# The order of VectorE's work in the second Y phase: weight rests behind the pair's work

## The chip, the cores and the metric

The kernel runs on one core of a Trainium2 chip. The metric is device time in microseconds. Several runs are taken and their median is compared; a run with the profiler gives the trace.

Five engines work beside each other, each in its own order: TensorE (PE) multiplies matrices, VectorE (DVE) and ScalarE (ACT) work element by element, GpSimd (POOL) issues some of the transfers and does a few small operations, SyncE (SP) issues most of the transfers. Semaphores make one engine wait for another or for a transfer.

## The reference, cut to what matters

Two batches of 1024 rows with 1024 columns go through a layer normalization, two products and a gate. `S` is a product with a block-sparse weight, `Y` a product with a dense weight plus a mix of eight low-rank terms whose coefficients come from the mean over the rows:

```python
xn = layernorm(x)
s = xn @ (weight * block_mask).T + bias
coeffs = softmax((mean_over_rows(xn) @ Wq.T) @ lora_keys.T / sqrt(128))
y = xn @ (W_org.T + sum_e coeffs[e] * down[e] @ up[e])
out = x + s * silu(y)
```

## The kernel before, in words

**Precision.** Every float32 operand of a product is kept as two parts: the part rounded to the type that TensorE multiplies (written by ScalarE, `hi`) and the rest, operand minus rounded part (written by VectorE, `lo`). A product is three matmuls: hi by hi, hi by lo, lo by hi. The *rest* of this document's title is the `lo` part of a block of the S weight.

**Stages.** Batch 0 is computed in the plain way: S's left half, Y's left half (phase `("y", 0, 0)`), Y's right half (phase `("y", 0, 1)`, the *second Y phase*, 157 to 204 us), then S's right half in eight tiles (`s_tile`), mixed with *folds*, which make the Y weight of batch 1. Batch 1 is computed with a scheme of seven products in place of eight on 2 by 2 blocks (from about 291 us to the end); it needs sums and differences of blocks of the normalized input, made ahead of time and stored in DRAM (`xv`).

**The second Y phase.** TensorE computes eight tiles of 128 rows, 24 matmuls each (`gemm`, L450 to L454). Beside it three other tasks run, which the generator `jobs_c(i)` hands out tile by tile:

- *S weight, right half*, eight blocks `kt` of 128 by 512. `s_mul` (L294 to L303): SyncE loads the block into a stage tile `ws` (L297), VectorE multiplies it by the block mask (L299), ScalarE writes the rounded part into `slot` (L302). `s_lo` (L305 to L307): VectorE writes the rest, block minus rounded part, into `slot` (L307); this frees the stage tile. The result, `s1`, is first used by `s_tile(0)`.
- *Pairs of blocks of batch 1's input*. `wide_load` (L958) loads two blocks in a pair `j`; `wide_norm` subtracts the row means (L962) and scales, while it sums each row (L963, sums into `xsum`); `wide_a(j)` normalizes the first half, `wide_b(j)` the second half and then forms four differences (L968), whose stores to `xv` GpSimd issues (L524). Pair 0 and half of pair 1 belong to the phase before; `wide_b(1)`, `wide_a(2)`, `wide_b(2)`, `wide_a(3)`, `wide_b(3)` to tiles 0 to 4 of this phase. Pair 3 uses the tiles of pair 1 again.
- *The coefficients of batch 1* (`coeffs(1)`, four steps). `steps[0]`, `sums`: eight transposes of `xsum` on TensorE (L322), behind the matmuls of tile 5. `steps[1]`, `query`: VectorE multiplies the sums by `Wq` (L346) and makes `qb` (L350). `steps[2]`, `scores`: TensorE multiplies `qb` by the keys (L357); this stands in the middle of tile 6 (`split_at`), between its first twelve matmuls and the rest; then VectorE begins the softmax (L359 to L362). `steps[3]` ends it, and `scale_up` scales the low-rank factors for the folds (L389 to L393).

**What sets the order.** TensorE, VectorE, ScalarE and GpSimd run exactly in the order in which the program is written (`manual_schedule`). SyncE is not in that list: a planner orders its loads. A load waits in its queue until its tile is free, and what is behind it waits too. Stage tiles come from one pool of six (`tag="st"`), which `ws`, the fourth difference of a pair (`xt`) and the fold's loads (`ds`, `wo`, `us`) share. `unit_load` (L1081) loads batch 1's first unit of weights into `raw`, parts of which hold the row means and pair 2's second half in this phase.

Of the kernel before, what the change touches and what calls it, by code (L numbers as in the profile page):

```python
# [32 lines left out]
def kernel(  # L33
# [258 lines left out]
    def new_slot():  # L292
        return wpool.tile([P, NKT, 2, NH], F32R, name="slot", tag="w")
# [257 lines left out]
    J = lambda f, *a: (lambda: f(*a))  # L551
# [98 lines left out]
    with tc.manual_schedule(engines={mybir.EngineType.PE, mybir.EngineType.DVE, mybir.EngineType.Activation, mybir.EngineType.Pool}):  # L650
# [343 lines left out]
        s1 = new_slot()  # L994
        steps = coeffs(1)

        def jobs_c(i):
            if i < 2:
                yield J(store_out, 1 - i)
            if i == 5:  # L1000
                yield steps[0]
                yield steps[1]
            if i == 6:
                yield steps[3]
                yield J(scale_up, 1, 0, up_homes)
            if i < 6:
                yield J(s_mul, s1, 1, i)
                yield J(s_lo, s1, 1, i)
            if i == 5:
                for kt in (6, 7):  # L1010
                    yield J(s_mul, s1, 1, kt)
                    yield J(s_lo, s1, 1, kt)
            if i in (0, 2):
                yield J(wide_load, 2 + i // 2, 0)
                yield J(wide_load, 2 + i // 2, 1)
            if i < 5:
                yield J((wide_b, wide_a)[i % 2], 1 + (i + 1) // 2)

        up_homes = [misc[:, 0, :]]
        split_at[(0, 1, 6)] = steps[2]  # L1020
        phase("y", 0, 1, y01, False, jobs_c)


# [341 lines left out]
```

## Time and profile before

| | us |
|---|---|
| three runs, median (lowest to highest) | 453.02 (452.56 to 454.11) |
| the profiled execution | 451.54 |
| its span, first to last instruction | 449.8 |
| TensorE busy (98% of the span) | 439.7 |
| VectorE busy (64%) | 289.4 |
| ScalarE busy (39%) | 175.6 |
| GpSimd busy (17%) | 76.6 |
| from 186 to 198 us: TensorE busy, of 12 | 10.25 |
| from 186 to 198 us: VectorE busy, of 12 | 10.23 |

The page and the views give each instruction's line in the kernel, its engine, its tiles (output, arrow, inputs), its start and its duration. A bracket behind a row of the timeline is the idle time of that engine just before, and what ended it. In the list of waits a row reads: the waiting instruction, an arrow, what it waited for, then the total, the number of times and the longest. The granted clock of TensorE was 1.00 in every stretch of the second Y phase. Matmul durations overlap (a matmul of 512 columns is shown as 0.39 us long, but the next starts 0.23 us after it).

### The profile page before, as it was taken

To read this page: it belongs to the slowest core of one execution; us is meant where nothing else is said; L and a number is where in the kernel's file an instruction comes from. 1 tells how busy PE (TensorE), PEld (TensorE's weight loads), DVE (VectorE), ACT (ScalarE), POOL (GpSimd) and SP (SyncE) were. 2 spreads that over 40 slices of the span, in tenths; PEclk is the share of its full clock that TensorE was granted. 3 is DMA by queue.
4 is the path that set the end of the run, shared out by engine and by line. 5 is a ranking of instruction groups with operands and counts; after the bars stand their busy time and mean duration, and the time that the engine had idled before them with its cause. 6 is when DMAs were issued, how large, how long until landed. Compare 5 with 4: busy or idle time off the path is not lost.

```text
span 449.8 us, 5786 instructions
## 1 busy us (share of the span) xinstructions
PE 439.7 (98%) x2058; PEld 363.3 (81%) x2058; DVE 289.4 (64%) x478; ACT 175.6 (39%) x291; POOL 76.6 (17%) x93
## 2 busy tenths in 40 slices
PE   7999999999999999999999999999999999999996
PEld 5789888888888888778888788888888888888885
DVE  5989777766528758876456667487556294365615
ACT  3676626454631221225233134067344322441520
POOL 3784210002220402221000000110020030002000
PEclk9999999999999999999999999999999999999999
DMA  8995406687796887797979797966183146218103
GB/s 272 390 345 207 143 25 206 215 265 217 250 306 179 267 248 251 268 346 259 286 219 311 218 306 197 302 176 189 40 180 127 66 110 172 93 24 209 49 1 117
DMA packets 47741, 90.58 MB, mean 201 GB/s; under 512 B 4816, under 2 KB 15328, under 8 KB 47712
## 3 DMA queue, kind: packets, MB, share of 16 engines
q1 hardware_dynamic: 30624, 66.08, 43.1%
q0 software_dynamic: 6624, 16.26, 15.7%
q10 hardware_dynamic: 10464, 7.87, 5.4%
q8 instruction: 16, 0.26, 0.3%
q14 instruction: 13, 0.11, 0.1%
HBM read 70.26 MB, written 19.93 MB: 201 GB/s over the span
## 4 chain that ended last, share of the span: by engine, by line
PE 73%; issue 10%; DMA 8%; DVE 4%; POOL 3%; SPq 0%; ACT 0%; POOLq 0%; DVEq 0%; ACTq 0%
PE acc_ps L1211 25%; PE py L1211 10%; PE acc_ps L450 8%; PE acc_ps L454 8%; PE acc_ps L453 8%; PE psw L416 5%; PE psw L415 5%; PE psw L414 5%; DMA ramp<-in_wT_dram 2%; DMA keys_sb<-in_keysT_dram 2%; POOL xv L524 2%; DMA ramp<-in_mask_dram 2%; DMA misc<-in_up_dram 1%; DMA xv<-xt 1%; POOL stash L502 1%
## 5 line engine op out<-in xcount | busy, mean ns | idle before, releaser
L1211 PE MATMUL acc_ps<-xw,ow 128*128 128x512 f32 (+1 forms) x492 | 113.2, 386 | 0.0
L1211 PEld LDWEIGHTS acc_ps<-xw,ow 128*128 128x128 f32 x492 | 91.0, 188 | 19.5
L450 PE MATMUL acc_ps<-slot,xgrp 128*128 128x512 f32 (+1 forms) x288 | 106.6, 370 | 0.1
L454 PE MATMUL acc_ps<-slot,xgrp 128*128 128x512 f32 (+1 forms) x288 | 105.7, 367 | 0.7 <-DVE xgrp L603 0.7
L453 PE MATMUL acc_ps<-slot,xgrp 128*128 128x512 f32 (+1 forms) x288 | 105.7, 367 | 0.6 <-DVE slot L591 0.2
L453 PEld LDWEIGHTS acc_ps<-slot,xgrp 128*128 128x128 f32 x288 | 54.3, 189 | 10.8 <-DVE slot L591 2.1
L454 PEld LDWEIGHTS acc_ps<-slot,xgrp 128*128 128x128 f32 x288 | 54.2, 188 | 10.2 <-DVE xgrp L603 1.1
L450 PEld LDWEIGHTS acc_ps<-slot,xgrp 128*128 128x128 f32 x288 | 54.3, 189 | 9.1 <-DVE stash L466 0.3
L416 PE MATMUL psw<-cut,dlo 128*128 128x512 f32 x128 | 50.1, 391 | 0.3 <-DVE dlo L406 0.3
L414 PE MATMUL psw<-cut,dhi 128*128 128x512 f32 x128 | 49.9, 390 | 0.0
L415 PE MATMUL psw<-cut,dhi 128*128 128x512 f32 x128 | 49.8, 389 | 0.0
L1211 PE MATMUL py<-xw,ow 128*128 128x512 f32 x192 | 46.9, 392 | 0.0
L1211 PEld LDWEIGHTS py<-xw,ow 128*128 128x128 f32 x192 | 36.1, 188 | 7.9
L1104 DVE TENSOR_TENSOR ow<-raw,ow 128x1024 fp32r<-128x1024 f32 (+1 forms) x32 | 34.5, 1088 | 9.9 <-ACT ow L1103 9.9
L405 ACT CAST dhi<-ds 128x512 fp32r<-128x512 f32 x32 | 19.7, 616 | 40.8 <-DMA ds<-in_down_dram 25.2
L502 POOL DMA_DIRECT2D stash<-in_x_dram x16 | 14.4, 899 | 117.6 <-DVE stash L499 117.6
L421 DVE TENSOR_TENSOR wo<-wo,psw 128x512 f32<-128x512 f32 x32 | 21.9, 685 | 13.2 <-PE psw L416 13.0
L406 DVE TENSOR_TENSOR dlo<-ds,dhi 128x512 fp32r<-128x512 f32 x32 | 22.0, 687 | 12.6 <-ACT dhi L405 12.5
L1103 ACT CAST ow<-raw 128x1024 fp32r<-128x1024 f32 (+1 forms) x32 | 29.4, 941 | 1.8 <-DVE wo L421 1.6
L416 PEld LDWEIGHTS psw<-cut,dlo 128*128 128x128 f32 x128 | 24.0, 188 | 5.8 <-DVE dlo L406 0.9
L415 PEld LDWEIGHTS psw<-cut,dhi 128*128 128x128 f32 x128 | 24.1, 188 | 5.1
L414 PEld LDWEIGHTS psw<-cut,dhi 128*128 128x128 f32 x128 | 24.0, 188 | 4.9
(180 smaller groups left out, 468.9 us busy)
## 6 DMA issues: line engine op xcount, KB each, us to landing
ds<-in_down_dram SPq DMA_DIRECT2D x32, 256.0 KB, 3.7
wo<-in_worgT_dram SPq DMA_DIRECT2D x32, 256.0 KB, 3.7
raw<-in_x_dram SPq DMA_DIRECT2D x11, 512.0 KB, 4.9
stash<-in_x_dram POOLq DMA_DIRECT2D x16, 256.0 KB, 4.8
raw<-in_wu_dram SPq DMA_DIRECT2D x8, 512.0 KB, 4.9
yu<-wo ACTq DMA_DIRECT2D x16, 256.0 KB, 4.5
raw<-yu SPq DMA_DIRECT2D x8, 512.0 KB, 3.7
out_dram<-stash ACTq DMA_DIRECT2D x14, 256.0 KB, 4.1
```

The lines of the kernel that those rows point to most:

```text
L405: nc.scalar.copy(dhi, ds)
L406: nc.vector.tensor_tensor(dlo, ds, dhi.bitcast(F32), ALU.subtract)
L414: nc.tensor.matmul(ps, lhsT=dhi[:, c, :], rhs=u[c][:, 0, :], start=c == 0, stop=False)
L415: nc.tensor.matmul(ps, lhsT=dhi[:, c, :], rhs=u[c][:, 1, :], start=False, stop=False)
L416: nc.tensor.matmul(ps, lhsT=dlo[:, c, :], rhs=u[c][:, 0, :], start=False, stop=c == 3)
L421: nc.vector.tensor_tensor(ws, ws, ps, ALU.add)
L450: nc.tensor.matmul(ps, lhsT=xs[:, kt, 0, cols], rhs=w[:, kt, 0, wc], start=kt == 0, stop=False)
L453: nc.tensor.matmul(ps, lhsT=xs[:, kt, 0, cols], rhs=w[:, kt, 1, wc], start=False, stop=False)
L454: nc.tensor.matmul(ps, lhsT=xs[:, kt, 1, cols], rhs=w[:, kt, 0, wc], start=False, stop=kt == NKT - 1)
L1103: nc.scalar.copy(o[:, a:b, 0], raw[:, a:b])
L1104: nc.vector.tensor_tensor(o[:, a:b, 1], raw[:, a:b], o[:, a:b, 0].bitcast(F32), ALU.subtract)
L1211: nc.tensor.matmul(ps, lhsT=o[:, a, wl, j, :], rhs=xw[j][:, m, xl, cols], start=start and j == 0 and k == 0, stop=j == 3 and k == 2, skip_ ...
```

## The change

Only the order of jobs in `jobs_c` changes. For tiles 0 to 4 the rest (`s_lo`) of the tile's weight block stands behind the pair's work (`wide_a` or `wide_b`) instead of right behind the mask product. For tile 5 the mask product of block 5 stands ahead of the coefficient steps `sums` and `query` instead of behind them, and the last three blocks are done as two products and then three rests, instead of product and rest in turn.

```diff
@@ -997,24 +997,26 @@
         def jobs_c(i):
             if i < 2:
                 yield J(store_out, 1 - i)
+
+            if i < 6:
+                yield J(s_mul, s1, 1, i)
             if i == 5:
                 yield steps[0]
                 yield steps[1]
             if i == 6:
                 yield steps[3]
                 yield J(scale_up, 1, 0, up_homes)
-            if i < 6:
-                yield J(s_mul, s1, 1, i)
-                yield J(s_lo, s1, 1, i)
             if i == 5:
-                for kt in (6, 7):
-                    yield J(s_mul, s1, 1, kt)
+                yield J(s_mul, s1, 1, 6)
+                yield J(s_mul, s1, 1, 7)
+                for kt in (5, 6, 7):
                     yield J(s_lo, s1, 1, kt)
             if i in (0, 2):
                 yield J(wide_load, 2 + i // 2, 0)
                 yield J(wide_load, 2 + i // 2, 1)
             if i < 5:
                 yield J((wide_b, wide_a)[i % 2], 1 + (i + 1) // 2)
+                yield J(s_lo, s1, 1, i)
```

In VectorE's order of this phase, with m for a mask product, r for a rest, a and b for a pair's halves and q for the query:

```
before: m0 r0 b1 m1 r1 a2 m2 r2 b2 m3 r3 a3 m4 r4 b3 q m5 r5 m6 r6 m7 r7
after:  m0 b1 r0 m1 a2 r1 m2 b2 r2 m3 a3 r3 m4 b3 r4 m5 q m6 m7 r5 r6 r7
```

## The prediction

> **What bounds the kernel now.** I read the page first. Its busy table has TensorE at work for almost the whole span:
>
> ```profile
> span 449.8 us, 5786 instructions
> PE 439.7 (98%) x2058; PEld 363.3 (81%) x2058; DVE 289.4 (64%) x478; ACT 175.6 (39%) x291; POOL 76.6 (17%) x93
> ```
>
> So this change, which touches no matmul, can win no more than the stalls that TensorE has near it. The list of waits, for TensorE from 160 to 300 us, holds three:
>
> ```profile
> PE sp L357 <- DVE qb L350: 1.1, 1, 1.1
> PE xrow L322 <- DVE bd L963: 0.7, 1, 0.7
> PE psw L416 <- DVE dlo L406: 0.3, 1, 0.3
> ```
>
> The first two lie in the second Y phase, and VectorE ends both. Their price is read better from TensorE's timeline (start, duration, instruction):
>
> ```profile
> 189.41 0.93 PE L322 MATMUL xrow<-ident,xsum 128*128 128x128 f32 x7
> 191.00 0.32 PE L322 MATMUL xrow<-ident,xsum 128*128 128x128 f32 x1 [0.67 <-DVE bd L963]
> ...
> 193.71 0.39 PE L454 MATMUL acc_ps<-slot,xgrp 128*128 128x512 f32 x1
> 195.18 0.36 PE L357 MATMUL sp<-keys_sb,qb 128*128 128x8 f32 x2 [1.08 <-DVE qb L350]
> ```
>
> Seven transposes in 0.93 us are 0.133 each, so the eighth was due at 190.34 and ran at 191.00: 0.66 lost. Matmuls of 512 columns follow each other every 0.2275 us, so the score matmul was due at 193.71 + 0.23 = 193.94 and ran at 195.18: 1.24 lost. Together **1.90 us**; that is the stake.
>
> Why VectorE is late is in its timeline, of which these rows carry the phase:
>
> ```profile
> 161.95 0.68 DVE L299 TENSOR_TENSOR ws<-ws,m_sb 128x512 f32<-128x512 f32 x1
> 164.93 0.69 DVE L307 TENSOR_TENSOR slot<-ws,slot 128x512 fp32r<-128x512 f32 x1 [2.29 <-ACT slot L302]
> 165.54 1.22 DVE L962 TENSOR_TENSOR bd<-bd,raw 128x1024 f32<-128x1024 f32 x1
> ...
> 182.09 0.69 DVE L299 TENSOR_TENSOR ws<-ws,m_sb 128x512 f32<-128x512 f32 x1 [0.24 <-DMA ws<-in_wT_dram]
> 183.47 0.69 DVE L307 TENSOR_TENSOR slot<-ws,slot 128x512 fp32r<-128x512 f32 x1 [0.69 <-ACT slot L302]
> ...
> 188.47 1.22 DVE L962 TENSOR_TENSOR bd<-bd,raw 128x1024 f32<-128x1024 f32 x1
> ...
> 193.40 0.68 DVE L346 SCALAR_TENSOR_TENSOR junk<-xrow,misc 128x512 f32<-128x512 f32 x1
> ...
> 195.26 0.69 DVE L299 TENSOR_TENSOR ws<-ws,m_sb 128x512 f32<-128x512 f32 x1 [0.23 <-DMA ws<-in_wT_dram]
> ```
>
> Each rest (L307) waits for ScalarE's rounding of the product just made: 2.29 us for weight 0, because ScalarE was itself held until 164.28 behind an output store, and 0.69 for each later one. Nothing else holds VectorE up to the last row sum (the read of L963's accumulator, done at 190.95) but 0.24 for a load. Last, SyncE's timeline:
>
> ```profile
> 173.41 0.33 SPq L958 DMA_DIRECT2D ac<-in_xT_dram  x1
> 174.87 0.33 SPq L958 DMA_DIRECT2D bd<-in_xT_dram  x1
> 175.25 1.43 SPq L297 DMA_DIRECT2D ws<-in_wT_dram  x2
> 186.16 3.88 SPq L1081 DMA_DIRECT2D raw<-in_wu_dram  x2
> 190.14 1.32 SPq L297 DMA_DIRECT2D ws<-in_wT_dram  x3
> ```
>
> The weight loads stand behind others in this queue: weights 3 and 4 behind pair 3's loads, which wait until pair 1's sums are stored (its tiles are used again); weights 5 to 7 behind the first unit's load into raw, whose second half waits for the last mean subtraction (L962, ended 189.69). The reader should keep this last row: it decides the order of VectorE's new waits.
>
> **The change, part by part.** It adds and removes no instruction. SyncE's loads keep their program order, and the order in which the stage tiles are asked for is the same. I take SyncE's issue order as before.
>
> *Rests 0 to 4 behind the pair's work.* Durations, start to start: a product or a rest 0.61; the longer half of a pair (wide_b) 4.93 (165.54 to 170.47); the shorter (wide_a) 2.40 (172.46 to 174.86). The load of pair 1's second half was issued at 154.91 and took 6.7, so it was there at 161.6, and the first wide_b can start at 161.95 + 0.61 = 162.56, 2.98 earlier than 165.54. It ends at 167.49; rest 0 and product 1 give 168.71; wide_a 171.11; rest 1 and product 2 172.33; the second wide_b 177.26; rest 2 177.87. The rounded parts are ready by then, since ScalarE has whole pairs of time for each.
>
> Product 3 now meets its load. Pair 1's store starts 2.98 earlier, so the loads behind it do: weight 3's at 172.27 instead of 175.25. That load was met at 182.09, 6.8 after issue; so 179.1, a wait of 1.2 where 0.24 was (pair 3's own loads, 5.8 and 6.5 long and also 2.98 earlier, are there before they are needed). The extra running ahead is lost here, but the 2.98 stay. From there: product 3 done 179.7, wide_a 182.1, rest 3 and product 4 183.3, mean subtraction of the last half done at 184.55, **last row sum at 185.8** (2.48 after the start, as before), instead of 190.95. TensorE wants it at 190.34: the 0.66 go, with 4.5 to spare.
>
> *Weight 5's product ahead of the query.* This is the part that costs. Before, the query (L346, L350) ran at 193.40 to 195.03 while weight 5's load was still under way. Now the differences end at 188.25, rest 4 at 188.85, and the product must be done first. Its load leaves 0.45 after the last mean subtraction (189.69 to 190.14), now at 185.0. It was met 5.1 after issue: 190.1. So VectorE waits 1.25, the product ends at 190.7, and the query, 1.63 long, gives qb at 192.35; TensorE follows 0.14 later (195.04 to 195.18), at 192.5. TensorE itself comes at 189.41 + 8 x 0.133 + 12 x 0.2275 = 193.2. So the 1.24 go too, with **0.7 to spare**.
>
> That load's duration is the uncertain price. On L297 the eight loads took 3.2 to 8.5. At 3.2 nothing changes; at 8.5 the product waits until 193.5 and TensorE stands 193.5 + 0.61 + 1.63 + 0.14 - 193.2 = 2.7, which is 0.8 worse than now in sum. I take 5.1, since the same load, behind the same two transfers and with pair 3's stores starting the same 3.1 after its issue (193.29 before, 188.1 now), took that. The trace shows what crowding does: the two loads of stored sums issued at 194.1 and after, into pair 3's stores, took 8.3 and 9.5. [...]
>
> *Products 6 and 7, then rests 5 to 7.* Before, 195.26 to 201.21 with three waits of 0.69; now from 192.35: two products to 193.6, rest 5 to 194.2, rest 6 to 194.8, rest 7 after its rounding at about 195.5. The softmax behind them moves from 201.2 to about 195.5, and the tiles that these rests free for the fold loads come 4 to 5 us sooner. The first S tile begins at 203.6 (201.7 after) and needs rest 7 only at its end. No cost.
>
> *What is late next.* After the phase TensorE comes 1.9 earlier. The first fold, at 209.1 now, uses the scaled factors that VectorE ends at 208.0; TensorE will want them at 207.2, and they move with the softmax, some 5 us. The tightest later place is the third wait above, 0.3 at about 248, behind a chain that begins with TensorE's own matmul at 233.57, so it moves along.
>
> The sum: -0.66 - 1.24 = -1.90 against the profiled execution of 451.54 (span 449.8): 449.6. The median shown is 453.02, 1.5 above that execution, so I forecast 453.0 - 1.9 = **451.1**. A measurement can tell about 0.3%, 1.36 us, from no change.
>
> **Rivals.**
>
> 1. *Part of the query's wait stays.* Weight 5 lands late, since its load shares the engines with stores. At the 6.7 that weights 3 and 4 took it lands at 191.7, and TensorE waits 0.9: the gain is 1.0, 452.0. For it: the loads of this line took 6.5 or more in four of eight cases. Against it: the load in this very place took 5.1. Chance 0.17.
>
> 2. *The gain is given back later.* In the folds, VectorE works without a pause from 242 to 252 and TensorE already waits there; loads from 195 to 204 fill the DMA engines (share 1.0). If those chains do not move with TensorE, up to 1.9 comes back: 453.0. Against it: the chain starts at a TensorE instruction, and its loads leave earlier. Chance 0.11.
>
> 3. *It does not do what it says.* VectorE's waits for ScalarE become waits for loads (as at product 3), and the sums come no earlier: 453.0. That needs weight 3's load not to move with the store in front of it. Chance 0.04.
>
> 4. *Slower.* The same place as rival 1 with a larger price: weight 5 lands so late that the query's wait exceeds today's two stalls. Slower by 0.3% means a wait of 1.9 + 1.36 = 3.26, so a landing at 194.1, 9.1 after issue. No load of this line took that, but one into the stores did (9.5: TensorE waits 3.7, +1.8, 454.8). Chance 0.12.
>
> **How the numbers follow.** The forecast, both stalls gone, has 0.56. Faster is the forecast and a quarter of rival 1: 0.60. Same is the rest of rival 1 with rivals 2 and 3: 0.28. Slower: 0.12. The range: the forecast's own is 450.4 to 451.7, as each stall may be off by some tenths and the median by 0.5. Upward it reaches over rivals 1 to 3 to 453.4; downward to 450.0. That leaves out rival 4 and little more.
>
> **What would show it.** VectorE's timeline: the first wide_b at about 162.6, right behind product 0; rests without idle time; the last L963 at about 184.6 and a wait for a load before product 5, in front of L346. TensorE's waits: xrow and sp gone from the list. If sp is still there with some tenths or more, the row before L346 tells whether weight 5's load did it (rivals 1 and 4); if both are gone and the time is not, the waits after 203 us must have grown (rival 2). Wrong from the start would be SyncE issuing weights 3 and 4, or 5 to 7, in another place than behind the loads named.

## The result and the profile after

| | before | after |
|---|---|---|
| median, us (lowest to highest, runs) | 453.02 (451.59 to 455.74, 11) | 450.57 (448.64 to 452.20, 11) |
| ratio, 95% interval | 1 | 0.9944 (0.9922 to 0.9967) |
| the profiled execution | 451.54 | 452.20 |
| its span | 449.8 | 450.5 |

The change makes the kernel faster by 2.45 us; 451.1 was forecast. Timed again beside other kernels it had 450.74 (ratio 0.9959, 0.9936 to 0.9982).

The profiled execution, however, is no shorter than that of before. This is the first thing to learn here: one execution differs from the next by as much as the effect (4 us from lowest to highest), so a pair of traces must be compared stretch by stretch, and only the stretch that the change touches. In the whole:

```profile
span 450.5 us, 5791 instructions
PE 440.4 (98%) x2058; PEld 363.7 (81%) x2058; DVE 288.9 (64%) x478; ACT 175.7 (39%) x291; POOL 76.4 (17%) x93
```

Each of these engines has as many instructions as before; the five more in the first line are none of theirs.

TensorE's first matmul of the second Y phase starts at 156.76 before and at 157.14 after, so 0.38 was lost earlier, where nothing was changed. From there to the first matmul behind the score matmul it is 38.63 us before and 37.58 after: 1.05 won. From there to the end it is 254.44 and 255.75: 1.31 lost, of which TensorE's waits from 160 to 300 us show 0.9, the growth of the wait on dlo:

```profile
PE psw L416 <- DVE dlo L406: 1.2, 1, 1.2
PE sp L357 <- DVE qb L350: 0.9, 1, 0.9
```

The wait on xrow is gone, the one on qb is 0.9 where it was 1.1, and the wait on dlo near 248 us is 1.2 instead of 0.3. TensorE's timeline after:

```profile
189.78 1.03 PE L322 MATMUL xrow<-ident,xsum 128*128 128x128 f32 x8
...
193.18 0.39 PE L454 MATMUL acc_ps<-slot,xgrp 128*128 128x512 f32 x1
194.50 0.36 PE L357 MATMUL sp<-keys_sb,qb 128*128 128x8 f32 x2 [0.94 <-DVE qb L350]
```

All eight transposes now run in one go (x8). The score matmul was due at 193.18 + 0.23 = 193.41 and lost 1.09. VectorE's timeline of the phase after tells why:

```profile
162.18 0.69 DVE L299 TENSOR_TENSOR ws<-ws,m_sb 128x512 f32<-128x512 f32 x1
162.78 1.22 DVE L962 TENSOR_TENSOR bd<-bd,raw 128x1024 f32<-128x1024 f32 x1
...
167.72 0.68 DVE L307 TENSOR_TENSOR slot<-ws,slot 128x512 fp32r<-128x512 f32 x1
...
180.57 0.69 DVE L299 TENSOR_TENSOR ws<-ws,m_sb 128x512 f32<-128x512 f32 x1 [2.42 <-DMA ws<-in_wT_dram]
...
192.12 0.69 DVE L299 TENSOR_TENSOR ws<-ws,m_sb 128x512 f32<-128x512 f32 x1 [1.71 <-DMA ws<-in_wT_dram]
192.73 0.68 DVE L346 SCALAR_TENSOR_TENSOR junk<-xrow,misc 128x512 f32<-128x512 f32 x1
```

The first wide_b starts right behind product 0, and rest 0 (L307) has no bracket: it waits for nothing any more. But two products wait for their loads, product 3 for 2.42 us and product 5, in front of the query, for 1.71. SyncE's rows:

```profile
171.60 0.33 SPq L958 DMA_DIRECT2D ac<-in_xT_dram  x1
172.83 0.33 SPq L958 DMA_DIRECT2D bd<-in_xT_dram  x1
173.21 1.36 SPq L297 DMA_DIRECT2D ws<-in_wT_dram  x2
183.78 2.58 SPq L1083 DMA_DIRECT2D raw<-in_wu_dram  x2
186.45 1.33 SPq L297 DMA_DIRECT2D ws<-in_wT_dram  x3
```

The order is that of before. Pair 3's first load was 2.98 us earlier in the forecast and is 1.81 earlier here (2.04 if counted from VectorE's product 0, which starts 0.23 later in this trace).

### The profile page after: what moved, and what is told of

Same layout as the page of the kernel before. It is cut to its first block, busy times and chain, and to the rows that moved or that the text cites. A ratio compares the mean times of both kernels' runs of the same rounds, so it can differ in the third digit from the quotient of the medians.

```text
span 450.5 us, 5791 instructions
## 1 busy us (share of the span) xinstructions
PE 440.4 (98%) x2058; PEld 363.7 (81%) x2058; DVE 288.9 (64%) x478; ACT 175.7 (39%) x291; POOL 76.4 (17%) x93
## 4 chain that ended last, share of the span: by engine, by line
PE 68%; DVE 11%; DMA 11%; issue 6%; ACT 3%; POOL 1%; SPq 0%; ACTq 0%; DVEq 0%; POOLq 0%
PE acc_ps L1213 25%; PE py L1213 10%; PE acc_ps L454 7%; PE acc_ps L450 7%; PE acc_ps L453 7%; PE psw L416 4%; PE psw L414 4%; PE psw L415 4%; DMA ws<-in_wT_dram 3%; DMA stash<-in_x_dram 2%; DMA yu<-wo 2%; DVE st L145 1%; DVE slot L591 1%; DMA raw<-in_x_dram 1%; DMA raw<-in_mask_dram 1%
## 5 line engine op out<-in xcount | busy, mean ns | idle before, releaser
L1196 POOL DMA_DIRECT2D gate<-in_xT_dram x12 | 10.5, 909 | 94.2 <-DVE gate L1190 68.8
```

## The experiments

Two measures are used. The medians come from repeated runs. From each trace comes the time from TensorE's first matmul of the second Y phase to the first matmul behind the score matmul ("phase"), and from there to the end ("rest"):

| kernel | median, us | ratio to before (95%) | phase, us | rest, us |
|---|---|---|---|---|
| before (also f1, f3: three traces) | 453.0 | 1 | 38.63, 38.48, 39.12 | 254.4, 255.2, 255.3 |
| after (also f2, h3: three traces) | 450.57; 450.74 | 0.9944 (0.9922 to 0.9967); 0.9959 (0.9936 to 0.9982) | 37.58, 37.66, 38.21 | 255.8, 255.8, 254.9 |
| e1, rests only | 450.41 | 0.9940 (0.9923 to 0.9958) | 36.93 | 254.6 |
| e2, tile 5 only | 457.74 | 1.0103 (1.0077 to 1.0129) | 42.33 | 255.9 |
| e3, h4, query first | 450.11; 450.66 | 0.9931 (0.9904 to 0.9958); 0.9953 (0.9936 to 0.9969) | 36.41, 36.71 | 254.7, 255.3 |
| g1, query later by 1.2 | 453.73 | 1.0008 (0.9978 to 1.0037) | 38.82 | 255.6 |
| e4, query later by 2.4 | 456.50 | 1.0090 (1.0055 to 1.0125) | 40.53 | 257.2 |
| h1, e4 with its wait filled | 454.17 | 1.0037 (1.0018 to 1.0057) | 39.90 | 254.6 |
| h2, before with its wait filled | 452.70 | 1.0000 (0.9982 to 1.0017) | 38.67 | 254.6 |

Theory 1: the time follows TensorE's two waits in the second Y phase. Theory 2, the rival: what the change wins comes from what is freed earlier behind the query, and the two waits are given back later.

**Each half alone.** Rests 0 to 4 behind the pair's work, tile 5 as before (order m4 b3 r4 q m5 r5 m6 r6 m7 r7; the diff is against before, cut):

```diff
             if i < 6:
                 yield J(s_mul, s1, 1, i)
-                yield J(s_lo, s1, 1, i)
             if i == 5:
+                yield J(s_lo, s1, 1, 5)
...
             if i < 5:
                 yield J((wide_b, wide_a)[i % 2], 1 + (i + 1) // 2)
+                yield J(s_lo, s1, 1, i)
```

> Only the first half of the change: rests 0 to 4 stand behind the pair's work; tile 5 is as before (query, then product and rest in turn). Theory 1, the time follows TensorE's two waits in the second Y phase (on xrow and on qb) one for one: both waits gone, as nothing with a load of its own stands in front of the query; gain over before 1.9 us or a little more than the full change, 451.1 us, ratio 0.995 to 0.996. Theory 2, the gain comes from what is freed earlier behind the query (softmax, fold loads), and the two waits are given back at TensorE's later wait on dlo near 248 us: products and rests 5 to 7 in turn are about 1 us later than in the full change, so about half to two thirds of its gain, ratio about 0.997, and the wait near 248 us grows by what the two waits lose.

It has the whole gain, 2.6 us (interval 1.9 to 3.5, where 1.9 was expected), and its trace has neither wait: the phase is 36.93 us, 1.70 shorter than in the first trace of before. The wait near 248 us, which theory 2 wants grown, is not in its list at all.

Tile 5 alone (m4 r4 b3 m5 q m6 m7 r5 r6 r7), rests 0 to 4 right behind their products (against before, the new lines):

```diff
+            if i < 6:
+                yield J(s_mul, s1, 1, i)
+            if i < 5:
+                yield J(s_lo, s1, 1, i)
             if i == 5:
                 yield steps[0]
                 yield steps[1]
...
+                yield J(s_mul, s1, 1, 6)
+                yield J(s_mul, s1, 1, 7)
+                for kt in (5, 6, 7):
+                    yield J(s_lo, s1, 1, kt)
```

> Only the second half of the change: rests 0 to 4 stand right behind their products as before; in tile 5 the product of weight 5 stands ahead of the query, and products 6 and 7 ahead of rests 5 to 7. Theory 1: the wait on xrow stays at 0.66 us, and the query waits for weight 5's load (met at 195.26 us before), so qb comes at about 197.5 instead of 195.0 and the wait on qb grows from 1.2 to 3.7 us: slower than before by about 2.5 us, 455.5 us, ratio 1.005 to 1.006. Theory 2: the softmax and the fold loads move by under 0.5 us against before, so no change, ratio 1.000.

Slower by 4.7 us: theory 2 is out, and theory 1 has only about half of it. TensorE's waits in its trace and VectorE's product 5:

```profile
PE sp L357 <- DVE qb L350: 4.0, 1, 4.0
PE xrow L322 <- DVE bd L963: 1.2, 1, 1.2
```
```profile
197.53 0.69 DVE L299 TENSOR_TENSOR ws<-ws,m_sb 128x512 f32<-128x512 f32 x1 [2.17 <-DMA ws<-in_wT_dram]
198.14 0.68 DVE L346 SCALAR_TENSOR_TENSOR junk<-xrow,misc 128x512 f32<-128x512 f32 x1
```

The query stands behind product 5 and so behind its load, as the forecast said of this half. It is a loss that the first half pays for. What theory 1 lacks is in part the clock, of which more below: behind this wait the granted clock is 0.83 from 198 to 201 us and 0.60 from 201 to 204, where 10 matmuls run instead of 15.

**The query ahead of everything it does not need** (b3 q r4 m5 m6 m7 r5 r6 r7; against the full change, cut):

```diff
-            if i < 6:
+            if i < 5:
                 yield J(s_mul, s1, 1, i)
             if i == 5:
                 yield steps[0]
                 yield steps[1]
+                yield J(s_lo, s1, 1, 4)
+                for kt in (5, 6, 7):
+                    yield J(s_mul, s1, 1, kt)
+                for kt in (5, 6, 7):
+                    yield J(s_lo, s1, 1, kt)
...
-                yield J(s_lo, s1, 1, i)
+            if i < 4:
+                yield J(s_lo, s1, 1, i)
```

> The change with the query ahead of everything that it does not need: pair 3's differences, query, rest 4, products 5 to 7, rests 5 to 7. Theory 1: no wait on xrow and none on qb (qb at about 192.5 us, TensorE there at 193.4); 1.9 us faster than before, and faster than the full change by the wait on qb that its profile still shows (0.94 us): ratio to before 0.993 to 0.996. Theory 2: softmax and fold loads stand as in the full change, so the same time as the full change, 0.9944, and the wait on dlo near 248 us takes up what the wait on qb loses.

Its VectorE timeline and its whole list of TensorE's waits from 160 to 300 us:

```profile
189.41 0.68 DVE L968 TENSOR_TENSOR xt<-bd,tt 128x512 f32<-128x512 f32 x1
191.84 0.69 DVE L346 SCALAR_TENSOR_TENSOR junk<-xrow,misc 128x512 f32<-128x512 f32 x1 [1.75 <-PE xrow L322]
...
193.18 0.29 DVE L350 TENSOR_TENSOR qb<-qh 128x128 f32<-128x128 f32 x1
```
```profile
PE psw L416 <- DVE dlo L406: 0.2, 1, 0.2
```

Now VectorE waits for TensorE in front of the query, not the other way round. The phase is 36.41 us, against 37.6 to 38.2 in the traces of the full change. To see whether the time follows, both were timed once more on one chip:

> The full change once more, timed beside h4 on one chip. Both of its traces have 0.95 us of wait on qb, which the kernel with the query first has not. If that wait is in the usual execution too, this kernel is 0.9 to 1 us slower than h4 (ratio to before about 0.996 against 0.994). If the traced executions are special in this, the two are equal within 0.3 us.

> The kernel with the query ahead of rest 4 and product 5 once more (as e3_query_first), timed beside h3: no wait on xrow or qb; 0.9 to 1 us faster than the full change by theory 1, equal to it by theory 2.

450.74 and 450.66: no difference, where the traces differ by 1.5 us in the phase (38.21 and 36.71). The full change's trace here has 1.6 us of wait on qb, but it is again of its slowest execution (454.4; the others go down to 449.3), and it stands 1.7 us behind the first trace of before already at 14 us. Both it and the second trace of the full change have a mean granted clock of 0.996, where its first trace has 0.999; the second ran at 0.50 from 9 to 12 us, far ahead of anything that the change touches. The wait on qb is in every trace of the full change, yet not visible in its median. Of the other executions only the time, the span and the mean granted clock are on record, so whether they have less of this wait is open.

**Further traces** of both kernels, with no edit:

> The kernel before once more, for a second trace. The full change gained 2.45 us at the median (interval 1.5 to 3.5) and its two stalls were 1.90 us in the one trace of before, an execution (451.54 us) near the fastest of its kernel. Theory 1 with larger stalls: in a usual execution the waits on xrow and qb are together longer than in that trace, about 2.5 us. Rival: they are 1.9 us again, and what the median gains beyond that lies after 203 us, in TensorE's wait on dlo near 248 us (0.3 us in that trace, then about 1 us).

> The kernel before a third time, as f1_before_again: waits on xrow and qb together about 2.5 us by theory 1 with larger stalls, 1.9 us by the rival.

> The full change once more, for a second trace. Its first trace, an execution of 452.2 us and so the slowest of its kernel, had 0.94 us of wait on qb, with weight 5's load met 5.7 us after its issue, and 1.2 us on dlo near 248 us. If these two are what varies from execution to execution, a usual execution has less of them: the wait on qb between 0 and 1 us, following weight 5's landing one for one, and the wait on dlo between 0 and 1.2 us.

Before: xrow 0.5 and qb 1.1 in the second trace, 1.2 and 1.1 in the third, 0.7 and 1.1 in the first. So the stake is 1.6 to 2.3 us by this list, and the 1.90 of the forecast lies inside. The wait on dlo is 1.2 in both, so its 0.3 in the first trace was luck, and the 1.2 after is no effect of the change. After: qb 1.0, dlo 1.2. Over all traces of these kernels, the wait on dlo is 0 to 1.2 whatever the lead: 1.1 in one trace of the kernel with the query first, 0.2 in the other. It is not where the gain is given back.

**The query made later.** Weight 5's mask product is repeated, which leaves the weight as it is:

```diff
-        nc.vector.tensor_tensor(
-            v, v, m_sb[:, kt, 16 * h : 16 * (h + 1)].unsqueeze(2).to_broadcast([P, 16, 32]), ALU.mult
-        )
+        for _ in range(5 if kt == 5 else 1):
+            nc.vector.tensor_tensor(
+                v, v, m_sb[:, kt, 16 * h : 16 * (h + 1)].unsqueeze(2).to_broadcast([P, 16, 32]), ALU.mult
+            )
```

> The full change, with weight 5's mask product done five times instead of once (the mask is 0 or 1, so the weight is the same): 2.4 us more VectorE work directly in front of the query. Theory 1: qb 2.4 us later and TensorE's wait on it 2.4 us longer (0.94 to 3.3 us); the time is 2.4 us above the full change, 453.0 us, ratio to before 1.000. Theory 2, the waits of this phase are given back later: the time rises by well under 2.4 us, ratio 0.995 to 0.997.

The phase grew by 2.3 to 3.0, as theory 1 has it, but the time by 5.9. TensorE's score matmul, and a table of stretches (the column behind POOL's is the granted clock):

```profile
197.23 0.57 PE L358 MATMUL sp<-keys_sb,qb 128*128 128x8 f32 x2 [3.69 <-DVE qb L351]
```
```profile
192.00:195.00 3.00, 1.54 (x7) 0.94 (x5) 2.86 (x5) 0.00 (x0) 0.00 (x0) 1.00 1.03 416
195.00:198.00 3.00, 0.77 (x3) 0.80 (x4) 2.96 (x8) 0.89 (x2) 0.00 (x0) 0.72 0.81 301
198.00:201.00 3.00, 3.00 (x8) 2.32 (x8) 2.57 (x7) 1.53 (x3) 0.28 (x1) 0.50 0.66 218
201.00:204.00 3.00, 3.00 (x10) 2.35 (x10) 0.78 (x4) 0.68 (x2) 1.39 (x1) 0.64 0.81 240
```

From 198 to 201 only 8 matmuls run instead of 15: the clock is at half. From 198.22 to 202.92 us a matmul starts every 0.43 us instead of 0.23, and with those at its two ends 2.6 us are lost. To tell the clock from a late query, the wait was filled with matmuls whose result nobody uses:

```diff
+        def filled_scores():
+            ps = ps_w.tile([P, NH], F32, name="psw", tag="psw")
+            for _ in range(14):
+                nc.tensor.matmul(ps, lhsT=xg[(0, 1)][:, 0, 0, :P], rhs=y01[:, 0, 0, :], start=True, stop=True)
+            steps[2]()
+
-        split_at[(0, 1, 6)] = steps[2]
+        split_at[(0, 1, 6)] = filled_scores
```

> e4_late_query with 14 extra matmuls (result unused) in TensorE's queue ahead of the score matmul: 3.2 us of work in the place where TensorE waits 3.7 us for qb. e4 cost 5.9 us over the full change where its VectorE work is 2.4. If the surplus is the clock, which the trace of e4 shows at 0.50 after the wait, the filled wait keeps the clock at 1.00 and the time is that of the full change plus 2.4: 453.0 us, ratio to before 1.000, with 0.5 us left of the wait on qb. If the surplus comes from what the late query delays behind it, the time stays at 456.5 us, ratio 1.008.

2.3 of the 3.5 us of surplus are gone, with the mask product still done five times, and the stretches have the clock at 1.00:

```profile
195.00:198.00 3.00, 2.92 (x15) 2.15 (x13) 2.97 (x9) 1.47 (x4) 0.00 (x0) 1.00 0.94 341
198.00:201.00 3.00, 3.00 (x15) 2.49 (x14) 1.65 (x5) 0.62 (x2) 1.20 (x1) 1.00 0.57 147
```

So most of the surplus is the clock's. The 454.17 are 1.2 above the 453.0 expected, and no wait on qb is left where 0.5 was expected: that sum took for granted that the full change loses 0.95 us on qb anyway. Against 450.6 the kernel is 3.5 slower, about the 3.2 that the filling lasts. That fits a usual execution with little wait on qb, as the equal times of h3 and h4 do, but does not prove it.

Half the dose (`range(3 ...)` in the same place), and the kernel before with five such matmuls ahead of its score matmul:

> The full change with weight 5's mask product done three times: 1.2 us more VectorE work in front of the query, half of what e4_late_query added (which cost 5.9 us over the full change in place of 2.4, with the granted clock at 0.5 to 0.7 for some 6 us after a wait of 3.7 us). If the surplus there comes from the clock and needs a wait of about that length, this kernel's wait on qb is 1.2 us longer than the full change's (about 1.5 to 2.2 us), the clock stays at 1.00 and the time is 1.2 us above the full change: 451.8 us, ratio to before 0.997. If the surplus grows with every wait, in proportion, it is 2.9 us above the full change: 453.5 us, ratio 1.001.

> The kernel before with 5 extra matmuls (1.14 us, result unused) ahead of the score matmul, where its traces show TensorE waiting 1.1 us on qb. It removes no wait on VectorE. If part of the 2.5 us that the change gains beyond its 1.9 us of stalls is a lower clock after these stalls in executions that were not traced, this kernel is faster than before by up to 0.6 to 1 us, ratio 0.998. If the clock plays no part in before, the same time or up to 0.1 us more, ratio 1.000.

The median of the half dose answers to neither case: its trace has a wait of 2.2 and the clock at 1.00, yet the median rose by 3.1, with runs from 451.3 to 457.3, wider than any other kernel's. The mean granted clock of each of its twelve executions takes them apart. Five have 0.999 or 1.000 and a median of 452.2, 1.6 above 450.6, near the 1.2 of the first case. Four have 0.996 (453.4 to 454.6) and three 0.992 or 0.993 (456.2 to 457.3); the traced execution of e2, with a lowered clock in two stretches of 3 us, has 0.996, and that of e4, with one in three stretches, 0.992. Of the 23 timed executions of the full change two have 0.996, none has less. So some executions lose the clock and others do not, and those that lose it make the surplus. Where in the execution they lost it is not on record. Before, filled: the same time. The clock plays no part that can be measured in before, and 1.14 us of matmuls put in front of the score matmul cost nothing that can be measured, as there was a wait of that size.

## Why the prediction was right, step by step

- *The stake* of 1.90 us, two waits of TensorE on VectorE: right. With both gone from the trace (e1, e3, h4) the phase is 1.7 to 2.2 us shorter than in the first trace of before, and the medians of the three timings are 2.2 to 2.9 lower.
- *Rests 0 to 4 behind the pair's work*: right. The first wide_b starts 0.60 behind product 0; no rest waits; the last row sum is there at 187.3 (forecast 185.8) instead of 190.95, before TensorE's need, and the 0.66 on xrow are gone.
- *Product 3 meets its load*: right in kind, too small. Forecast 1.2 us, measured 2.42. The forecast let the store of pair 1's sums, which pair 3's load waits for, move by the same 2.98. It took 3.9 us instead of 3.0, and started 2.8 earlier (167.61) it met the output store that ScalarE issued at 166.41 and that landed at 170.3 (the DMA engines' share is 0.74 from 168 to 171); before, the DMA engines were nearly idle (share 0.02 from 168 to 171) when it started. That the output store is the cause is argued from this pair of traces, not shown. Weight 3's load itself then took 7.3 instead of 6.8. So the work that ran ahead met another transfer here.
- *The query's 1.24 with 0.7 to spare*: failed in the traces. Weight 5's load left at 186.45 instead of 185.0 (the 1.2 us of slip above, and a phase that starts 0.2 later on VectorE) and was met 5.7 after its issue instead of 5.1, while TensorE came 0.2 later: 0.7 to spare turned into 1.09 lost. That is rival 1, with its price of about 1 us: the traces gain 1.0 in the phase, not 1.9. In the medians the gain is 2.45 and 2.07, which the forecast's 1.9 fits better than rival 1's 1.0; the interval of the second, 0.8 to 2.9, does not exclude 1.0. Why the traces are worse than the medians is open: two of the three had lost time near the start, but that does not touch the phase. So the time came out as forecast although this step is not borne out by any trace of the change, and as far as the traces are typical that is luck.
- *What is late next, the wait at 248*: it does move along with TensorE, but its 0.3 was not typical: 0.3 to 1.2 in three traces of before, 0.2 and 1.1 in two of the kernel with the query first. Rival 2 is out.
- *SyncE's issue order as before*: right, so rival 3 is out.
- *Rival 4, slower by the same place*: its mechanism is real, as the second half alone shows (4.7 us slower). It needed a wait of more than 3.26 by one-for-one counting; with the clock, which the forecast did not price, the wait of 3.7 in e4's trace cost 2.6 more.

## What to carry to other kernels

On an in-order engine, put work whose inputs are ready in front of an instruction that waits for another engine, and put what the bottleneck waits for ahead of everything it does not need: the query in front of product 5 removes the same waits without a load in its way. Its time (450.1 and 450.7) cannot be told from the change's, but its trace has the margin that the change lacks. Price such a margin in transfers that move too, since pair 3's load, which waits for a store, came only 1.81 us earlier here, although the store started 2.76 earlier.

## What the runs showed of the hardware

In e4 a wait of TensorE cost more than its length. Around and behind its 3.7 us the granted clock is 0.72, 0.50 and 0.64 in the three stretches of 3 us from 195 to 204, with matmuls every 0.43 us instead of 0.23. Behind the 4.0 us of e2 it is 0.83 and 0.60 from 198 to 204, and with the wait of e4 filled (h1) it is 1.00 from 186 to 207.

The length of the wait alone does not decide in these traces. Behind the half dose's 2.2 us the clock stays at 1.00 (every stretch to 207 us). Near the start of the kernel, 1.59 us in the first trace of before leave it at 1.00 too (from 6 to 12 us), but 2.03 us in the second trace of the full change are followed by 0.50. TensorE's rows (before, then the full change's second trace) and a stretch of that second trace:

```profile
7.59 1.36 PE L206 MATMUL pt<-ident,acc 128*128 128x128 f32 x8 [1.59 <-ACT acc L163]
8.26 1.82 PE L206 MATMUL pt<-ident,acc 128*128 128x128 f32 x8 [2.03 <-ACT acc L163]
```
```profile
9.00:12.00 3.00, 3.00 (x10) 2.53 (x10) 2.15 (x5) 2.42 (x5) 0.56 (x1) 0.50 1.10 381
```

So of two waits of some 2 us one was followed by a lower clock and the other was not, which fits the half dose's spread. What decides between them is not shown.
